# A gated layer and its FFN in one kernel: early items of the down stage one step sooner, fold transposes handed out with their block's first product, byte stores ordered behind sums

## The chip, the cores and the metric

The kernel runs on one core of a Trainium2 chip. Its engines are named as in the profile: PE (TensorE matmul), PEld (its weight load), DVE (VectorE), ACT (ScalarE), POOL (GpSimd), SP (SyncE, which issues the DMAs). The metric is the device time of one execution in microseconds (us), as the median of several runs.

## The reference, cut to what matters

There are 2 x 1024 rows of H = 1024, in float32. A gated layer with a top-k mask comes first, then an FFN whose weights are repeated four times and carry an addition of rank 2. A layer norm follows each.

```python
s = silu(x @ w_gate.T)                       # rows x 2752
_, idx = top_k(-abs(s), 2752 // 2)           # the half that is smallest in size
s[rows, idx] = 0
x = layernorm(x + (s * (x @ w_up.T)) @ w_down.T)

def lin(x, wq, A, B):                        # w is wq side by side four times
    return x @ tile(wq, (1, 4)).T + (x @ A.T @ B.T) * 0.5
x = layernorm(x + lin(silu(lin(x, w1q, a1, b1)) * lin(x, w3q, a3, b3), w2q, a2, b2))
```

## The kernel before, in words

**Numbers as pairs.** Each float32 operand of a product is split in a high part and a low part (`wh`, `wl`; `xh`, `xl`; `mh`, `ml`; `fh`, `fl`; `hh`, `hl`). Three products (high by high, high by low, low by high) stand for one. ACT or POOL writes a high part (`split`, L171 and L173 for weights), POOL or DVE subtracts it from the whole for the low part (L174).

**Stage 1, `gate_up`,** takes about 929 us. The 16 tiles of 128 rows go in four groups `g` of four tiles, the 2752 columns in four pairs `u` of blocks of 344. Each (g, u) has gate steps (w = "g", seven products of block matrices, or eight for the first) and up steps (w = "u", k = 0 to 3). A step of `products` is 96 matmuls of 344 columns (L353). Results go through DRAM: `s_d` for the gate, `m_d` for gate times up (L387). Between the steps a generator `topk(g - 1)` hands out the work that finds the k-th size in each row; it ends with a byte mask for each tile that SP stores to `k_d` (L539).

**Early items.** In the last up steps (g = 3, u = 3) the generator `down(0, early=3)` is started and stepped: it loads, masks and transposes the first 512 columns of three tiles into tiles of their own, `em`, `eh`, `el` (`self.et`), so that stage 2 finds its first three items ready. `down_prep` makes four transposes an item (L745), ACT copies them to `eh` (L749), DVE subtracts to `el` (L750).

**Stage 2, `down`,** lasts from 929 to about 1466 us: four groups of four tiles, and in each six blocks of columns (`DB`: 512, 512, 512, 384, 384, 448). An item is one tile in one block: load of `m` (L710) and of the byte mask `u` (L711), ACT's conversion `ub` (L724), POOL's multiplication (L725), transposes (L745, L747), products of 512 columns (L765), and DVE's addition to `acc` (L768), which was loaded with x (L775). The weights `wd` are loaded at L603, split, and in the first group stored as pairs (L679). The top-k work of the last group runs beside the first groups of this stage, on ACT and DVE. The PSUM tiles named `mm` come from a pool of three.

**Stage 3, `ffn(g)`,** lasts to the end. As the FFN's weights repeat four times, a row's four quarters are added first: `f1_tile` loads the row tile, folds it on POOL (L927 to L929, buffer `fold`, one of it) and writes a small tile `tl` with the rank-2 terms (L938 to L940, one buffer); for tiles 12 to 15 it also makes the four dot products of the rank-2 term (DVE L925, buffer `pr`, and ACT L926). `f1_tile2` transposes both (PE L949, L951), and ACT and DVE write `fh` (L954) and `fl` (L955). Then come eight blocks `b` of 344 columns: `f1_mm` makes seven products for each of gate and up (L981 to L984), silu (L987), their product (L988), its rank-2 terms (L990, L992), and POOL adds blocks of the same parity to `hf` (L994). Last, `f2_prep` transposes `hf` (L1026, L1031) into `hh` (L1028) and `hl` (L1029), and `f2_mm` makes the second product (L765), the norm and the store. In group g the `f1_tile` and `f1_tile2` of group g + 1's tiles are called, one of each in every second block.

**What sets the order.** `item(load, prep, mm, a1, a2)` calls `load` at once and hands out `prep` and `mm` later: an item waits behind `a1` others for its `prep`, and then behind `a2` others for its `mm`. In the FFN's first product both are 2, so the products of a tile are handed out four items, which is one block, after the block's loads. What is called outside an item is handed out where the program stands, ahead of the products still in the queues. But the order in which the instructions stand on each engine at the end is not that of the calls: a scheduler that plays the program's time line through writes it, within the dependences and the buffers. `issue_after` (with `load_behind` and `behind`) adds only an order between two instructions: `load_behind` puts an instruction behind the last load of `m`, `behind` puts it behind the last split of a down item on DVE and ACT.

Of the kernel before, what the change touches and what calls it, by code (L numbers as in the profile page):

```python
# [26 lines left out]
NU = NB // 2  # L27
# [5 lines left out]
GT = 4  # L33
# [32 lines left out]
class Kern:  # L66
# [216 lines left out]
    def gate_up(self):  # L283
        nc, V = self.nc, self.nc.vector
        ng = self.nt // GT
        self.steps = [(g, u, w, k) for g in range(ng) for u in range(NU) for w in "gu" for k in range(7 if w == "g" and g + u else 4)]
        self.xfull, self.tkg, self.xs, self.xraw, self.wraw, self.wq, self.li, self.wi = {}, None, {}, {}, [], [], 0, 0
        cc, self.b0 = {}, {}
        pss = {}
        xg = self.x_raw(0)  # L290
        next(xg)
        for i, (g, u, w, k) in enumerate(self.steps):
            while self.li < min(i + LOADS + 1, len(self.steps)):
                self.w_load(self.li)
                if self.li == 0:
                    list(xg)
                self.li += 1
            while self.wi < min(i + AHEAD + 1, len(self.steps)):
                j = self.steps[self.wi]
                if j[:2] == (0, 0):  # L300
                    for op in {("g", 0): ("A11", "A21"), ("g", 1): ("A12", "A22")}.get(j[2:], ()):
                        self.x_slot(op)
                self.w_prep(self.wi)
                self.wi += 1
            wh, wl = (x.rearrange("p (a b) -> p a b", a=KH) for x in self.wq.pop(0))
            if self.form(i):
                a = GATE[k][0]
                ps = self.pair()[:, :, :BW]
                self.products([(ps[:, p], self.xs[p, a]) for p in range(NPR)], wh, wl, True, True)
                self.post((g, u), k, ps, cc)  # L310
            else:
                first = w == "g"
                h = int((G0 if first else UP)[k][1]) - 1
                n = int((G0 if first else UP)[k][2]) - 1
                st, sp = (k < 2, k > 1) if first else (h == 0, h == 1)
                if st:
                    ps = [self.pair()[:, :, :BW] for j in range(2)]
                    pss[n] = ps
                ps = pss[n]
                for j in range(2):  # L320
                    self.products([(ps[j][:, p], self.xs[p, f"A{j + 1}{h + 1}"]) for p in range(NPR)], wh, wl, st, sp)
                if sp:
                    (self.up if w == "u" else self.gate)((g, u), n, ps, cc)
            if g + u == 0 and w == "u" and k:
                with self.behind():
                    for op in (("S2",), ("S1", "S3"), ("S4",))[k - 1]:
                        self.x_slot(op)
            if u == NU - 1 and g + 1 < ng:
                if (w, k) == XAT["raw"][0]:
                    self.xg = self.x_raw(g + 1)  # L330
                for _ in range(XAT["raw"].count((w, k))):
                    next(self.xg, None)
                for op in XAT.get((w, k), ()):
                    with self.behind():
                        self.x_slot(op)
            if g and (u, w, k) == TKAT:
                self.tkg = self.topk(g - 1)
            for _ in range(2 if w == "u" and k % 2 == 0 else 1):
                if self.tkg:
                    next(self.tkg, None)  # L340
            if (g, u, w) == (ng - 1, NU - 1, "u") and k > 1:
                next(self.d0)
            if (g, u, w, k) == (ng - 1, NU - 1, "u", 1):
                self.et = [self.tk.tile([P, NI], d, tag=f"a{j}", name=n) for j, (n, d) in enumerate((("em", F), ("eh", R), ("el", R)))]
                self.d0 = self.down(0, early=3)
                next(self.d0)
# [70 lines left out]
    def topk(self, g, nact=3):  # L417
        nc, tk, sm = self.nc, self.tk, self.sm
        V = nc.vector
        tiles = range(g * GT, (g + 1) * GT)  # L420
# [5 lines left out]
        b = ku.rearrange("p a n -> p (a n)").bitcast(F)  # L426
# [26 lines left out]
        for p in range(NPASS):  # L453
            for j in range(nact):
# [3 lines left out]
                with self.behind():  # L458
                    t, s = cur[:, 0, j : j + 1], cur[:, 1, j : j + 1]
                    nc.scalar.activation(jk.bitcast(I8), av[j], AF.Sign, bias=t, scale=-1.0, accum_out=s)  # L460
                    if m < GT:
                        t, s = cur[:, 0, m : m + 1], cur[:, 1, m : m + 1]
# [14 lines left out]
            t = nxt[:, 0]  # L477
# [57 lines left out]
        self.lastd = self.lastv = self.lasta = self.lastp = None  # L535
        for j, t in enumerate(tiles):
            yield
            with self.tc.issue_after(self.lastd.ins) if self.lastd is not None else ExitStack():
                nc.sync.dma_start(self.k_d[t], kv[j])  # L539

    def exact(self, a, kp, b, v, x, c, bit, half):
# [312 lines left out]
    def ffn(self, g):  # L854
        tiles = [t for t in range(g * GT, (g + 1) * GT) if t < self.nt]
        for b in range(NB):
            ws = []
            if tiles[-1] + 1 < self.nt:
                if b % 2 == 0:
                    if b:  # L860
                        self.f1_tile2(tiles[-1] + b // 2)
                    self.f1_tile(tiles[-1] + 1 + b // 2)
            for t in tiles:
                self.item(
                    lambda: self.f1_prep(b, ws),
                    lambda: None,
                    lambda st=self.fst[t], b=b, ws=ws: self.f1_mm(st, b, ws),
                    2, 2,
                )
        if tiles[-1] + 1 < self.nt:  # L870
            self.f1_tile2(tiles[-1] + GT)
        ws = []
        for t in tiles:
            self.item(
                lambda: self.f2_w(ws),
                lambda t=t: self.f2_prep(self.fst[t], t),
                lambda st=self.fst[t], t=t, ws=ws: self.f2_mm(st, t, ws),
                2, 1,
            )

# [211 lines left out]
```

## Time and profile before

| | |
|---|---|
| median of 3 runs | 1923.64 us (1919.69 to 1924.59) |
| the profiled execution's own time | 1926.91 us |
| its span, first to last instruction | 1925.1 us |
| mean granted TensorE clock | 0.993 |
| PE busy | 1885.3 us (98%), 10825 instructions |
| DVE, ACT, POOL busy | 1229.6, 904.0, 973.0 us |
| moved by DMA | 488.66 MB, mean 254 GB/s |

The span is that of one profiled execution and is compared with that execution's own time, not with the median. A share of busy time is a mean over three stages that have different limits, so the stretch around a change has to be looked at by itself: by a table of windows, by the waits with what released them, and by the timeline. "PEclk" is the share of full clock that TensorE was granted. Where a wait is for several things, the profile names the one that came last by its records.

### The profile page before, as it was taken

To read this page: it belongs to the slowest core of one execution; us is meant where nothing else is said; L and a number is where in the kernel's file an instruction comes from. 1 tells how busy PE (TensorE), PEld (TensorE's weight loads), DVE (VectorE), ACT (ScalarE), POOL (GpSimd) and SP (SyncE) were. 2 spreads that over 40 slices of the span, in tenths; PEclk is the share of its full clock that TensorE was granted. 3 is DMA by queue.
4 is the path that set the end of the run, shared out by engine and by line. 5 is a ranking of instruction groups with operands and counts; after the bars stand their busy time and mean duration, and the time that the engine had idled before them with its cause. 6 is when DMAs were issued, how large, how long until landed. Compare 5 with 4: busy or idle time off the path is not lost. (4 is left out here: it accounts for less than half of the span.)

```text
span 1925.1 us, 29381 instructions
## 1 busy us (share of the span) xinstructions
PE 1885.3 (98%) x10825; PEld 1754.4 (91%) x10825; DVE 1229.6 (64%) x1831; ACT 904.0 (47%) x1448; POOL 973.0 (51%) x606
## 2 busy tenths in 40 slices
PE   9999999999999999999999999999998999998998
PEld 9999999999999999999888787888787979898896
DVE  4633556767358574691238998688467857779565
ACT  4333477414883258622246533323333746557362
POOL 5655664445445354355565443554565746436062
PEclk9999999999999999999999999999999999999999
DMA  7677687676977868667798756977776878485651
GB/s 266 237 250 260 236 325 261 210 272 253 330 231 241 314 235 303 236 228 256 282 328 285 270 188 227 337 245 261 268 250 244 279 284 321 155 318 177 229 196 66
DMA packets 166205, 488.66 MB, mean 254 GB/s; under 512 B 24772, under 2 KB 45380, under 8 KB 166056
## 3 DMA queue, kind: packets, MB, share of 16 engines
q1 hardware_dynamic: 165848, 486.43, 71.9%
q8 instruction: 85, 1.39, 0.3%
q14 instruction: 64, 0.52, 0.1%
q10 hardware_dynamic: 208, 0.31, 0.0%
HBM read 370.30 MB, written 116.33 MB: 253 GB/s over the span
## 5 line engine op out<-in xcount | busy, mean ns | idle before, releaser
L174 POOL TENSOR_TENSOR wl<-wr,wh 128x1376 fp32r<-128x1376 f32 (+2 forms) x187 | 566.4, 3035 | 466.1 <-ACT wh L173 436.8
L353 PE MATMUL mm<-wh,xh 128*128 128x344 f32 x1928 | 610.4, 322 | 2.8 <-DMA wh<-tw3T1h 2.8
L353 PE MATMUL mm<-wh,xl 128*128 128x344 f32 x1928 | 609.8, 320 | 0.0
L173 ACT CAST wh<-wr 128x1376 fp32r<-128x1376 f32 (+2 forms) x192 | 232.4, 1215 | 340.9 <-PE mm L353 199.6
L353 PEld LDWEIGHTS mm<-wh,xh 128*128 128x128 f32 x1928 | 364.7, 189 | 3.0 <-issue 3.0
L353 PEld LDWEIGHTS mm<-wh,xl 128*128 128x128 f32 x1928 | 364.6, 189 | 0.0
L353 PE MATMUL mm<-wl,xh 128*128 128x344 f32 x1928 | 342.1, 319 | 0.0
L353 PEld LDWEIGHTS mm<-wl,xh 128*128 128x128 f32 x1928 | 310.1, 188 | 0.0
L765 PE MATMUL mm<-wh,mh 128*128 128x512 f32 x680 | 217.8, 400 | 0.1
L765 PE MATMUL mm<-wl,mh 128*128 128x512 f32 x680 | 215.1, 395 | 1.1 <-POOL wl L174 1.1
L765 PE MATMUL mm<-wh,ml 128*128 128x512 f32 x648 | 205.5, 396 | 0.8 <-DVE ml L750 0.8
L460 ACT ACTIVATE jk<-a,cur 128x2752 int8<-128x2752 f32 x66 | 170.8, 2588 | 31.2 <-DVE cur L482 15.8
L994 POOL TENSOR_TENSOR hf<-hf,gt 128x344 f32<-128x344 f32 x96 | 142.2, 1491 | 75.6 <-DVE gt L988 68.7
L725 POOL TENSOR_TENSOR m<-m,ub 128x512 f32<-128x512 f32 (+2 forms) x93 | 111.0, 1194 | 128.0 <-ACT ub L724 65.8
L981 PE MATMUL mm<-wh,fh 128*128 128x344 f32 x512 | 166.2, 325 | 5.8 <-DVE gt L988 5.2
L983 PE MATMUL mm<-wh,fl 128*128 128x344 f32 x512 | 164.0, 320 | 0.0
L982 PE MATMUL mm<-wl,fh 128*128 128x344 f32 x512 | 163.9, 320 | 0.0
L765 PEld LDWEIGHTS mm<-wl,mh 128*128 128x128 f32 x680 | 127.4, 188 | 30.1 <-POOL wl L174 2.2
L768 DVE TENSOR_TENSOR acc<-acc,mm 128x1024 f32<-128x1024 f32 x96 | 116.4, 1214 | 57.9 <-PE mm L765 27.8
L765 PEld LDWEIGHTS mm<-wh,mh 128*128 128x128 f32 x680 | 124.7, 189 | 24.8 <-ACT mh L749 0.5
L765 PEld LDWEIGHTS mm<-wh,ml 128*128 128x128 f32 x648 | 121.2, 189 | 26.9 <-DVE ml L750 1.0
L992 ACT ACTIVATE pa<-pa 128x344 f32<-128x344 f32 x256 | 123.0, 483 | 38.6 <-DVE pa L990 34.0
(191 smaller groups left out, 2742.5 us busy)
## 6 DMA issues: line engine op xcount, KB each, us to landing
wr<-wu SPq DMA_DIRECT2D x64, 688.0 KB
wr<-wg SPq DMA_DIRECT2D x52, 688.0 KB
wr<-wd SPq DMA_DIRECT2D x48, 512.0 KB
s_d<-cc SPq DMA_DIRECT2D x64, 344.0 KB
m_d<-mt SPq DMA_DIRECT2D x64, 344.0 KB
a<-s_d SPq DMA_DIRECT2D x64, 344.0 KB
wl<-wc_w SPq DMA_DIRECT2D x48, 344.0 KB
wh<-wc_w SPq DMA_DIRECT2D x48, 344.0 KB
```

What stands on the lines that cost most here:

```text
L173: self.lasta = self.nc.scalar.copy(hi, raw)
L174: (eng or self.nc.gpsimd).tensor_tensor(lo, raw, hi.bitcast(F), ALU.subtract)
L353: self.nc.tensor.matmul(o, l, r, start=start and n < m and n % (2 * KH) == 0, stop=stop and n >= m and (n - m) % KH == KH - 1)
L460: nc.scalar.activation(jk.bitcast(I8), av[j], AF.Sign, bias=t, scale=-1.0, accum_out=s)
L725: nc.gpsimd.tensor_tensor(m[:, :w], m[:, :w], ub[:, :w], ALU.mult)
L765: nc.tensor.matmul(ps[:, h], a, b[:, h * 512 : (h + 1) * 512], start=i == 0, stop=i == len(ops) - 1)
L768: nc.vector.tensor_tensor(out, out, ps.rearrange("p a b -> p (a b)"), ALU.add)
L981: nc.tensor.matmul(o, fh[:, c, :], wh[:, c, :], start=c == 0, stop=False)
L982: nc.tensor.matmul(o, fh[:, c, :], wl[:, c, :], start=False, stop=False)
L983: nc.tensor.matmul(o, fl[:, c, :], wh[:, c, :], start=False, stop=False)
L992: nc.scalar.activation(pa[:, r], pa[:, r], AF.Copy, scale=0.5, accum_out=part[:, r, b : b + 1])
L994: G.tensor_tensor(hf[:, hs], hf[:, hs], gt, ALU.add)
```

## The change

Three edits. In `gate_up` the early generator is made at k = 0 and stepped at k = 1 and 2, where it was made at k = 1 and stepped at k = 2 and 3. In `topk` the store of a byte mask is ordered behind the last load of `m` and behind the last split of a down item on DVE and ACT, where it was ordered behind the load alone. In `ffn` the calls of `f1_tile2` and `f1_tile` for the next group's tiles are put in a list `pre`, and the first product of the block that is handed out calls what is in it; the last `f1_tile2` is called with the first product of `f2_mm`. The same functions are called, with the same arguments. In the file after the change the lines from `ffn` on have numbers lower by one.

```diff
-            if (g, u, w) == (ng - 1, NU - 1, "u") and k > 1:
+            if (g, u, w) == (ng - 1, NU - 1, "u") and k in (1, 2):
                 next(self.d0)
-            if (g, u, w, k) == (ng - 1, NU - 1, "u", 1):
+            if (g, u, w, k) == (ng - 1, NU - 1, "u", 0):
                 self.et = [self.tk.tile([P, NI], d, tag=f"a{j}", name=n) for j, (n, d) in enumerate((("em", F), ("eh", R), ("el", R)))]
                 self.d0 = self.down(0, early=3)
                 next(self.d0)
...
         for j, t in enumerate(tiles):
             yield
-            with self.tc.issue_after(self.lastd.ins) if self.lastd is not None else ExitStack():
+            with self.load_behind(), self.behind():
                 nc.sync.dma_start(self.k_d[t], kv[j])
...
         for b in range(NB):
             ws = []
-            if tiles[-1] + 1 < self.nt:
-                if b % 2 == 0:
-                    if b:
-                        self.f1_tile2(tiles[-1] + b // 2)
-                    self.f1_tile(tiles[-1] + 1 + b // 2)
+            pre = []
+            if tiles[-1] + 1 < self.nt and b % 2 == 0:
+                if b:
+                    pre.append(lambda b=b: self.f1_tile2(tiles[-1] + b // 2))
+                pre.append(lambda b=b: self.f1_tile(tiles[-1] + 1 + b // 2))
             for t in tiles:
                 self.item(
                     lambda: self.f1_prep(b, ws),
                     lambda: None,
-                    lambda st=self.fst[t], b=b, ws=ws: self.f1_mm(st, b, ws),
+                    lambda st=self.fst[t], b=b, ws=ws, pre=pre: ([pre.pop(0)() for _ in pre[:]], self.f1_mm(st, b, ws)),
                     2, 2,
                 )
-        if tiles[-1] + 1 < self.nt:
-            self.f1_tile2(tiles[-1] + GT)
+        pre = [lambda: self.f1_tile2(tiles[-1] + GT)] if tiles[-1] + 1 < self.nt else []
         ws = []
         for t in tiles:
             self.item(
                 lambda: self.f2_w(ws),
                 lambda t=t: self.f2_prep(self.fst[t], t),
-                lambda st=self.fst[t], t=t, ws=ws: self.f2_mm(st, t, ws),
+                lambda st=self.fst[t], t=t, ws=ws, pre=pre: ([pre.pop(0)() for _ in pre[:]], self.f2_mm(st, t, ws)),
                 2, 1,
             )
```

## The prediction

> **What bounds the kernel now.** I read the page first, then the waits of TensorE, then a table by windows, then the timeline where a window is low.
>
> ```profile
> PE 1885.3 (98%) x10825; PEld 1754.4 (91%) x10825; DVE 1229.6 (64%) x1831; ACT 904.0 (47%) x1448; POOL 973.0 (51%) x606
> ```
>
> TensorE is busy 98% of 1925.1 us; the rest, 39.8 us, is all that moving work can win, plus what the halved clock costs. Where it lies:
>
> ```profile
> core 0: us, PE busy (x) PEld busy (x) DVE busy (x) ACT busy (x) POOL busy (x), PEclk, DMA share, GB/s
> ...
> 930.00:950.00 20.00, 16.66 (x69) 13.28 (x68) 4.76 (x7) 6.05 (x10) 13.72 (x8) 0.83 0.96 359
> ...
> 1050.00:1100.00 50.00, 48.70 (x229) 39.73 (x228) 48.39 (x91) 28.43 (x33) 20.31 (x16) 1.00 0.77 284
> ...
> 1450.00:1500.00 50.00, 45.10 (x238) 40.04 (x237) 38.95 (x97) 24.41 (x58) 24.24 (x33) 0.93 0.72 250
> ...
> 1550.00:1600.00 50.00, 47.19 (x233) 39.55 (x232) 30.27 (x74) 17.97 (x48) 15.87 (x25) 0.97 0.76 297
> ...
> 1700.00:1750.00 50.00, 48.09 (x309) 47.52 (x308) 48.51 (x74) 38.48 (x117) 27.63 (x25) 1.00 0.80 275
> ```
>
> The row 930–950, where stage 2 begins, loses most: PE busy 16.66 of 20, clock 0.83. 1450–1500 and 1550–1600 are FFN rows. In 1050–1100 and 1700–1750 the column DVE is 48.4 of 50: no room there. What ends the waits:
>
> ```profile
> PE mm L765 <- ACT hh L1028: 4.4, 3, 2.8
> PE tp L745 <- POOL m L725: 4.3, 2, 2.7
> PE tp L949 <- POOL fold L929: 3.2, 2, 1.9
> PE mm L745 <- DVE el L750: 1.9, 1, 1.9
> ```
>
> And the timeline at the start of stage 2, then at the FFN's start (start, length, engine and line, and in brackets the idle time before and its releaser):
>
> ```profile
> 929.54 1.03 PE L745 MATMUL mm<-ident,em 128*128 128x128 f32 x8
> 932.47 0.63 PE L745 MATMUL mm<-ident,em 128*128 128x128 f32 x4 [1.90 <-DVE el L750]
> 934.54 1.19 PE L765 MATMUL mm<-wh,eh 128*128 128x512 f32 x2 [1.45 <-POOL wl L174]
> 935.54 1.05 PE L765 MATMUL mm<-wl,eh 128*128 128x512 f32 x2
> ...
> 1481.06 0.44 PE L949 MATMUL tp<-ident,fold 128*128 128x128 f32 x2 [1.87 <-POOL fold L929]
> ...
> 1482.23 0.42 PE L981 MATMUL mm<-wh,fh 128*128 128x344 f32 x1 [0.51 <-DVE hf L988]
> ```
>
> The last up product starts at 929.4; then come the twelve transposes of the early items, in two lots, and the first down product at 934.54. The releaser "POOL wl" of that one is a guess of the view: in the built program it needs the third el from DVE (933.75–934.44), which needs eh, which needs the last four transposes.
>
> **The change, part by part.** Both built programs have equal counts of instructions on each engine. Their orders differ in two stretches only, about 922 to 1115 us and from 1478 on.
>
> **1. Early items one k sooner.** Eight of the twelve transposes move ahead of the second-last group of 24 products, four to six products into the last. ACT's eh and DVE's el follow them at about 923–927; they have all they need (their masks ended at 906 on POOL, the PSUM buffer was released at 915.55). The last el is done some 2 us before the last up product. So the first down product follows products: 929.54 + 12 x 0.109 (a transpose at its step) = 930.85, in place of 934.54: -3.69. Then the clock: the seven pairs of 512-column products from 934.54 on take 6.05 us to 940.59, where at the 0.231 step of full clock 14 need 3.23: -2.82 if the halved clock goes too.
>
> Here a rule speaks against the change. The Trainium skill, "TensorE: Matmul & The Clock Gate", Part 1: The HAM clock gate, says that the clock is halved after at least one idle window of about 3.4 us, and the table in its "Why this matters for your kernels" asks only for no gap over some 3 us. The row has 1.90 and 1.45, so by this rule the clock did not fall for these gaps, and -2.82 is not to be had. But its Part 4: PE-mode transpose says that transposes don't count as busy in the same way; then all from 929.54 to 934.54 is one quiet stretch of 5.0 us. The trace sides with that: clock 0.5 from 933.7 to 940.5, and a single gap of 2.7 us at 1188 with products on both sides left it at 1.00. In the new order eight transposes in a row are 0.87 us. I take -2.82; by the first rule the sum below is 2.8 worse.
>
> New wait: PE now reaches the fourth down item, which needs an mm buffer back, after 72 products and 8 transposes: 930.85 + 17.5 = 948.4. The buffer is freed by DVE's L768, which took 1.22 us and waits for the load acc<-x: issued at 940.72, landed at 947.04 (6.3 us, with the DMA engines at 0.96). In the new order that issue stands behind a weight load that waits for POOL's last splits, which wait for the last up product: about 1.1 later. So 948.1 + 1.2 = 949.4: +1.0 (0 to 3).
>
> Behind this the queues differ: on SP the wd loads come ahead of m, u and topk's a<-s_d (L440), on ACT and POOL the splits (L173, L174) stand ahead of the masks (L724, L725) that were before them, by 5 to 10 us. Following the chains by hand to 985, I find POOL's masks done 4 to 8 us ahead of their transposes: m at 956.9 for 961.8, 962.9 for 967.9, 968.4 for 976. Behind 1050 DVE is the narrow place: 97% busy, with topk passes of 3.07 us (L463) between the adds L768 (1.21) that free PSUM. There PE may have to hand back what it won. Bounds 0 and +5.5; I take +1, as TensorE still waited only 1.3 us in that window.
>
> Sum of part 1: -3.7 - 2.8 + 1.0 + 1.0 = -4.5.
>
> **2. Byte stores of the top-k bound.** The stores L539 stand in the same place on SP with the same waits in both built programs: 0. Were they moved, 64 KB loads u<-k_d are what waits for them, in other groups' masks.
>
> **3. Folds with the first product.** The code asks for all four fold groups of the next tiles later, but the written order moves just the last group of each block of four tiles: on PE from 1481 to about 1565, 1615 to 1672, 1722 to 1773. The first move doesn't pay on the spot: the product at 1482.23 needs DVE's hf (1481.66), and DVE's work ahead of it stays, so instead of 1.87 + 0.44 + 0.51 there is one gap of about 3.0, with the clock still halved; and four transposes (0.44) come back among products in f2. What it may win is at f2's start, where PE waits 2.81 for hh at 1554.62: ACT's fh (L954, 0.6) and DVE's fl (0.41) now stand behind hh. So hh is 0.6 to 1.0 sooner, and 1.8 of half clock behind that gap may go: -0.6 to -2.8. Group 1: 0 (its gap is 1.3). Group 2: the same 0.6 to 1.0, against the dots of tiles 13 to 15 (L925, four of 1.2 us a tile) that go one block later where DVE has no room: -1 to +3. I take -1.5 for all three, range -4 to +3. Cover: POOL and ACT are under 80% there; DVE is not, and that is the upper end.
>
> **Sum:** -4.5 + 0 - 1.5 = -6.0, against the profiled execution's own 1926.9 (span 1925.1 and 1.8 around it). That execution lies 3.3 over the median of 1923.64, and a shift carries over: 1917.6. About 0.3% (5.8 us) is what a measurement of this kernel can tell from no change, so this stands on the edge.
>
> **The rivals.**
> **Handed back** (chance 0.30). PE arrives 5.5 us sooner at a stage whose adds and masks are paced by DVE at 97% and by DMA at 0.96 and 0.91. For: those columns. Against: PE's own busy time in 950–1050 is 100%, so nothing was late there. If all of it goes back: +5.5 against the -6.5 +1.0, and the FFN's -1.5 stays: 1922.1.
> **The change doesn't do what it says** (inside both cases above). Two of its three parts nearly fall away in the written order; then part 1 alone carries it: 1919.1.
> **Slower: DVE's new order in 1000–1115** (chance 0.22). Where the topk passes fall differently, an add L768 can stand behind one more pass of 3.07 us, and PE, which has three mm buffers, stops until it is done. For: 1050–1100 has DVE at 48.39 of 50, and that stretch is rewritten. Against: with DVE as full as that, PE lost 1.5 us at 1072 in the order before, and nothing else between 1000 and 1115. Each such stop costs up to 3.07; beyond -6.0 the forecast turns at the second, and slower by 0.3% needs four. Five give +15.4 - 6.0 = +9.4, or with stops of 2.7, as the one at 1188, +7.5: 1931.
>
> **How the numbers follow.** Gain kept, -5.8 to -12 (chance 0.48): the upper end is no hand-back, no acc wait, and FFN -4. Handed back, within 0.3%: 0.30. Slower: 0.22. Range: below, 1911 is the forecast less the two +1 terms, and the FFN at -4, with a margin of 2 (0.07 left out); above, 1930 is just short of five stops (0.12 left out).
>
> **What would show it.** Right: ident,em in two lots ahead of 929, the first L765 at about 931, no clock of 0.5 in 933–940, and window 930–950 with PE over 19. The acc wait: PE before the fourth item's L765 idle about 1 us, released by L768. FFN: a gap of about 3 at 1479 less the shift; hh's 2.81 down to 2 or less. Wrong: clock 0.5 still there at the start of stage 2, or new lines "PE mm L765 <- DVE acc L768" of several us in 1000–1115, or hf and hh lines longer in the third FFN block.

## The result, and the profile after

The changed kernel takes 1930.95 us (median of 6 runs, 1927.42 to 1933.56), before takes 1921.51 us (6 runs, 1919.08 to 1924.59): ratio 1.0045, 95% interval 1.0031 to 1.0058. It is slower by some 9 us. The forecast was 1917.6.

The profiled execution of the changed kernel, at 1927.63 us, is one of its quickest, and that of before, at 1926.91 us, lay over all its six timed runs, so the two spans hardly differ. PE is still 98% busy (1885.5 us). So it has to be read stretch by stretch. The windows of the changed kernel, with the columns as above:

```profile
930.00:950.00 20.00, 20.00 (x98) 16.83 (x96) 1.57 (x2) 5.97 (x8) 14.08 (x8) 1.00 0.90 339
950.00:1000.00 50.00, 48.40 (x230) 39.58 (x229) 18.91 (x21) 21.30 (x29) 29.79 (x18) 1.00 0.94 347
1000.00:1050.00 50.00, 47.00 (x217) 37.87 (x217) 31.96 (x48) 29.87 (x36) 31.14 (x26) 1.00 0.79 277
...
1700.00:1750.00 50.00, 47.24 (x297) 46.06 (x297) 45.81 (x70) 38.02 (x115) 26.22 (x24) 1.00 0.74 245
1750.00:1800.00 50.00, 45.63 (x239) 39.49 (x238) 38.29 (x68) 26.66 (x82) 19.12 (x22) 0.97 0.38 124
```

Three of these windows before:

```profile
950.00:1000.00 50.00, 50.00 (x236) 41.03 (x235) 16.28 (x18) 19.34 (x27) 28.35 (x18) 1.00 0.91 328
1000.00:1050.00 50.00, 50.00 (x236) 40.95 (x236) 38.93 (x58) 31.63 (x40) 35.53 (x29) 1.00 0.86 292
...
1750.00:1800.00 50.00, 46.59 (x255) 40.91 (x254) 37.78 (x68) 27.39 (x84) 20.23 (x24) 1.00 0.41 128
```

In 930–950 PE is now busy all the time at full clock: what the forecast was after is there. But 950–1000 and 1000–1050, where PE lacked nothing before, lose 1.6 and 3.0 us, and both FFN windows lose about 0.9 more each; the last of them has lost full clock too (0.97). What ends PE's waits in the changed kernel:

```profile
PE mm L765 <- ACT hh L1027: 6.7, 3, 3.2
PE mm L980 <- DVE gt L987: 6.0, 8, 1.1
PE mm L765 <- ACT mh L749: 3.9, 4, 1.9
...
PE mm L980 <- DVE hf L987: 2.7, 1, 2.7
PE mm L765 <- DVE acc L768: 1.6, 1, 1.6
```

"el" and "m" are gone from the top; "mh" and "acc" are new, and "hh" has grown from 4.4. The timeline of PE shows each in its place:

```profile
929.47 0.60 PE L745 MATMUL mm<-ident,em 128*128 128x128 f32 x4
...
932.74 0.63 PE L765 MATMUL mm<-wh,eh 128*128 128x512 f32 x2
...
951.98 0.70 PE L765 MATMUL mm<-wh,mh 128*128 128x512 f32 x2 [1.60 <-DVE acc L768]
...
1023.88 0.73 PE L765 MATMUL mm<-wh,mh 128*128 128x512 f32 x2 [0.57 <-ACT mh L749]
...
1033.47 0.82 PE L745 MATMUL tp<-ident,m 128*128 128x128 f32 x6
1036.15 0.73 PE L765 MATMUL mm<-wh,mh 128*128 128x512 f32 x2 [1.86 <-ACT mh L749]
```

The first down product no longer waits (no bracket at 932.74). At 951.98 PE waits for its PSUM tile. From 1023 on an item's transposes stand right ahead of its products, and PE has nothing to do until ACT has written mh. Two of these waits, of 0.57 us, are the way over ACT alone. In the longest, 1.86 us at 1036.15, a load has a part as well. ACT's cast of a weight stands ahead of mh in ACT's order, and ACT sat idle for 2.54 us until the weight was there:

```profile
1034.68 1.04 ACT L173 CAST wh<-wr 128x1024 fp32r<-128x1024 f32 x1 [2.54 <-DMA wr<-wd]
1035.63 0.86 ACT L749 CAST mh<-tp 128x384 fp32r<-128x384 f32 x2
```

**One measure for all runs.** Below, "loss" is the sum, over PE's instructions in a stretch, of the time from one start to the next less the usual step of that shape (0.109, 0.157 and 0.231 us for 128, 344 and 512 columns). It holds idle time and halved clock alike; a stretch without a wait comes out at about -0.1. Each row is one profiled execution:

| kernel | 929–944 | 944–1020 | 1020–1060 | 1060–1120 | 1466–1562 | 1690–1790 |
|---|---|---|---|---|---|---|
| before | 6.5 | -0.1 | -0.1 | 1.5 | 13.6 | 7.4 |
| byte stores alone (before's order) | 5.3 | -0.1 | -0.1 | 1.4 | 15.1 | 7.5 |
| changed | 0.0 | 1.7 | 3.8 | 1.4 | 14.4 | 11.7 |
| changed, again | 0.0 | 4.0 | 4.5 | 1.4 | 14.2 | 11.5 |
| early edit alone | 0.0 | 3.7 | 5.4 | 1.4 | 13.9 | 7.5 |
| FFN edit alone | 6.4 | -0.1 | -0.1 | 1.9 | 14.7 | 11.6 |

The first two rows have one order of instructions, and so have rows three and four: they show what differs between executions of one order. Between 1120 and 1466, where the order is before's in all these kernels, the six executions differ by some 6 us in this measure (6.0 to 12.3), and no cause was read from there.

### The profile page after: what moved, and what is told of

Same layout as the page of the kernel before. It is cut to its first block, busy times and chain, and to the rows that moved or that the text cites. A ratio compares the mean times of both kernels' runs of the same rounds, so it can differ in the third digit from the quotient of the medians.

```text
span 1925.8 us, 29383 instructions
## 1 busy us (share of the span) xinstructions
PE 1885.5 (98%) x10825; PEld 1755.8 (91%) x10825; DVE 1223.8 (64%) x1831; ACT 905.9 (47%) x1448; POOL 974.0 (51%) x606
## 5 line engine op out<-in xcount | busy, mean ns | idle before, releaser
L460 ACT ACTIVATE jk<-a,cur 128x2752 int8<-128x2752 f32 x66 | 170.8, 2588 | 33.8 <-DVE cur L490 18.3
```

## The experiments

Times are medians. Ratios, with 95% intervals, are against runs of before on the same chip, whose medians are 1922.99 to 1923.57 us; a ratio differs by up to 0.0007 from that of the two medians. "F", "H" and so on are the theories that the expectations name.

**1. The parts, one by one.**

*The early edit alone:*

```diff
-            if (g, u, w) == (ng - 1, NU - 1, "u") and k > 1:
+            if (g, u, w) == (ng - 1, NU - 1, "u") and k in (1, 2):
...
-            if (g, u, w, k) == (ng - 1, NU - 1, "u", 1):
+            if (g, u, w, k) == (ng - 1, NU - 1, "u", 0):
```

> Before, with the first edit alone (early items made at k = 0, stepped at k = 1 and 2). Theory F (the loss lies in the FFN): this is faster than before by 2 to 6 us, about 1917, and its trace has no PE loss from 930 to 948 and the new one of about 6 us between 948 and 1115. Theory H (what is won at 930 is handed back twice over behind it): 3 to 9 us slower, 1925 to 1930.

Measured: 1925.38 us, ratio 1.0014 (1.0006 to 1.0022), slower by about 2.7. Theory F's time (about 1917) is ruled out, and theory H's is met at its lower edge (1925 to 1930): the gain is handed back and a little more, not twice over. Its waits from 929 to 1100, for which before's order has only el, wl and ml:

```profile
PE mm L765 <- ACT mh L749: 3.8, 4, 1.9
PE mm L765 <- DVE acc L768: 2.1, 1, 2.1
```

*The FFN edit alone* (the `pre` lists, as in the change):

```diff
-                    lambda st=self.fst[t], b=b, ws=ws: self.f1_mm(st, b, ws),
+                    lambda st=self.fst[t], b=b, ws=ws, pre=pre: ([pre.pop(0)() for _ in pre[:]], self.f1_mm(st, b, ws)),
```

> Before, with the FFN edit alone. Theory F: slower by 6 to 12 us, 1928 to 1933, with PE losing 5 us or more over before's 21.5 us from 1470 on. Theory H: within 2 us of before.

Measured: 1927.91 us, ratio 1.0028 (1.0019 to 1.0037), +5.4: most of the loss is the FFN's. That is just short of theory F's 6 to 12 and outside theory H's 2, so the loss has a share in both places.

*The byte stores alone:*

```diff
-            with self.tc.issue_after(self.lastd.ins) if self.lastd is not None else ExitStack():
+            with self.load_behind(), self.behind():
                 nc.sync.dma_start(self.k_d[t], kv[j])
```

> Before, with the edit of the byte stores alone. On each engine the order of instructions and their waits are those of before, so every theory expects 1921 within 2 us; it also gives a second profile of what is before's program, and so shows how far two executions of one order differ. If stores count after all: slower by over 5 us.

Measured: 1923.43 us, ratio 1.0000 (0.9989 to 1.0010). This part does nothing. Its profile serves below as a second one of before's order.

*The changed kernel on the same chip:*

> The changed kernel as it is, on the chip of the three others. 9 us slower than before (1930 to 1931); if the parts add up, its difference is the sum of those of the early edit and of the FFN edit within 3 us.

Measured: 1932.40 us, ratio 1.0042 (1.0024 to 1.0060). The parts add up: +0.0014 and +0.0028 give +0.0042.

**2. Why the early edit loses: lead.** In the written order of PE I counted the instructions between an item's last transpose and its first product, for the first twenty items after the early ones:

```
before               40 63 62 63 81 64 62 76 79 56 70 65 57 57 51 48 55 41 48 62
early edit, changed  10 29 45 21 25 40 44 61 67 57 51 32 18  1  1  4  5 10 27 23
```

Before, 40 or more instructions of PE cover the way from transpose over ACT to product. With the early edit the lead falls to 1 at the 14th item, and there, at 1023 to 1036, PE waits for mh. Why the scheduler's order has come to this was not followed. Theory L is that this is the loss; theory A, that PE has merely caught up with loads. The top-k work of the last group enters ACT's queue at item 12 of the group. Beginning it at item 16 restores the leads (10 29 45 21 25 40 47 64 70 82 76 67 61 61 57 57 57 30 25 36):

```diff
-                if g == 0 and n == 12:
+                if g == 0 and n == 16:
...
-                if (n > 11 or g) and self.tkg and next(self.tkg, 1):
+                if (n > 15 or g) and self.tkg and next(self.tkg, 1):
```

> The early edit alone, and the top-k work of the last group begins at item 16 of the first down group and not at item 12, so that its ACT passes come after the items that lost their lead. In the written order transposes then stand 30 to 80 PE instructions ahead of their products, where the early edit alone left 1 to 5 at items 14 to 17. Theory L (late transposes are what gives the gain back): the three waits for mh at 1024 to 1035 are gone, PE's loss from 948 to 1120 falls from 7.6 to 4 or less, time 3 to 5 us under the early edit alone, about 1921. Theory A (PE has only caught up with loads, whatever the order): the loss stays at 6 or more, time 1925.

> Before, with the top-k work begun at item 16 and not at item 12: the control for the run with the early edit. Leads there are long already, so both theories expect 1923 within 2 us; if beginning later pays or costs by itself, it shows here.

Measured: 1939.20 us with the early edit (1.0076, 1.0063 to 1.0089), 1944.43 us without (1.0106, 1.0091 to 1.0120). The expected times were wrong: beginning top-k later costs about 20 us by itself, much of it behind 1120: the loss from there to 1430 is 18.3 us in the control and 26.5 with the early edit (the slowest of its five runs), against 7.5 in the first profile of before. But against its own control the early edit now wins 5 us (1.0076 / 1.0106 = 0.9970), and from 930 to 1100 the waits for mh are gone:

```profile
PE mm L765 <- DVE acc L768: 2.7, 1, 2.7
PE tp L745 <- DVE num L488: 0.5, 1, 0.5
```

The loss at 1020–1060 is 0.0. Theory A would have kept it. What is left is the wait for acc, with 6.8 us of halved clock behind it, and it is large: 944–1020 loses 5.7. So from 948 to 1120 the loss is 6.5, where theory L wanted 4 or less, and from 929 to 1120 the two profiles lose the same (6.4 and 6.6). Where the 5 us are won doesn't show in them.

**3. Both losses taken out.** An item waits behind four others for its products in the first group (its transposes come one item sooner), and the first two acc loads are no longer ordered behind the loads of m:

```diff
-                    self.item(lambda: (load(), self.down_w(g, ib, ws)), prep, mm, 2, 3)
+                    self.item(lambda: (load(), self.down_w(g, ib, ws)), prep, mm, 2, 3 if g else 4)
...
-            with self.tc.issue_after(self.lastd.ins) if self.lastd is not None else ExitStack():
+            with self.tc.issue_after(self.lastd.ins) if self.lastd is not None and t > 1 else ExitStack():
                 self.nc.sync.dma_start(acc, self.A["x"][t * P : (t + 1) * P, :])
```

> The early edit alone, and in the first down group an item waits behind four others for its products, not three, so that transposes are handed out one item sooner; the top-k work begins where it did. Leads in the written order are 14 to 77 PE instructions, one of 6, in place of 1 to 67. Theory L (short leads): the waits for mh around 1024 to 1035 fall from 5.4 us to under 2, time about 1922. Theory A (caught up with loads): 1925 as with the early edit alone.

Measured, first edit on top of the early one: 1925.40 us, ratio 1.0003 (0.9991 to 1.0014). The time is theory A's number, the trace is not: the loss at 1020–1060 fell from 5.4 to 0.8, as theory L says, although ACT sat idle there for 3.6 us on the load of a weight; the longer lead covered that. But 1060–1120 rose from 1.4 to 6.5 (in the slowest of its 14 runs): there a top-k pass (L463) now stands on DVE ahead of ml and acc:

```profile
1079.31 3.07 DVE L463 TENSOR_SCALAR_CACHE_REDUCE ku<-a,cur 128x2752 uint8<-128x2752 f32 x1
...
1083.09 1.21 DVE L768 TENSOR_TENSOR acc<-acc,mm 128x1024 f32<-128x1024 f32 x1
1084.23 0.68 DVE L750 TENSOR_TENSOR ml<-tp,mh 128x512 fp32r<-128x512 f32 x1
```

and PE waits 1.56 us for that ml, with 6.8 us of halved clock.

> The early edit alone, and the first two loads acc<-x are not ordered behind the loads of m: on SP they stand 13 places sooner. The wait for acc L768 at about 950 (2.1 us, with the 1.5 to 1.9 us of halved clock behind it) goes, leads stay short (1 at items 15 and 16). Both theories expect 2 to 4 us under the early edit alone, about 1922.5, unless PE, let go at 950, then waits for mh there (the leads of the first two items are 5): then 1925.

Measured, second edit on top of the early one: 1923.31 us, ratio 0.9994 (0.9983 to 1.0005). The loads went out at 930.63 and 934.35, where the changed kernel has them at 943.84 and 944.91; the wait for acc and its halved clock are gone (944–1020: 0.3). Leads stay short and the loss there stays too (1020–1060: 7.1, of waits for mh and ml and 6.8 us of halved clock).

> Both of these on top of the early edit: the two acc loads sooner, and an item waits behind four others in the first down group. Theory L: nothing much is left of the loss behind 948, so PE's gain at 930 is kept: 1918 to 1920, faster than before by 3 to 5 us. Theory A: 1923 to 1925.

Measured, both: 1918.17 us, ratio 0.9968 (0.9956 to 0.9981): faster than before by about 6 us and than the changed kernel by about 14. Leads are 5 5 18 25 26 37 49 62 60 56 63 49 47 17 22 23 15 10 27 27. Its windows:

```profile
930.00:950.00 20.00, 20.00 (x98) 16.86 (x97) 4.03 (x5) 4.87 (x6) 12.90 (x7) 1.00 0.96 345
950.00:1000.00 50.00, 48.80 (x233) 39.75 (x232) 16.46 (x19) 22.89 (x32) 31.79 (x20) 1.00 0.98 363
1000.00:1050.00 50.00, 50.00 (x234) 40.81 (x233) 35.15 (x56) 29.88 (x36) 32.38 (x28) 1.00 0.82 288
```

The gain at 930 is there and 1000–1050 is whole again. It is what theory L expected (1918 to 1920). The two repairs together without the early edit were not run.

> Before, with four in place of three in the first down group: the control. Its leads were 40 to 80 and stay so: 1923 within 2 us.

Measured, the first edit on before: 1932.20 us, ratio 1.0045 (1.0026 to 1.0064). The control failed its expectation: with leads of 23 to 94 it is 9 us slower. 1060–1120 loses 5.1 (PE waits 2.2 for ml, behind a top-k pass again) and 1120–1300 loses 7.8, with one wait of 4.7 us for a mask; the latter is read in a single profile. So four in place of three is not good in itself, and a long lead is not all that counts.

**4. Why the FFN edit loses.** Group 2 differs from the others in that the tiles folded during it have dots on DVE, of 1.2 us each.

> Before, with the FFN edit in group 2 of the FFN alone (the one whose next tiles 12 to 15 need dots on DVE). Theory D (the dots one block later are the cost): +3 to +5 us over before, about 1927, with PE losing 11.5 us from 1690 to 1790 in place of 7.6. Theory G (each group costs its share): +1 to +2.

> Before, with the FFN edit in all groups but group 2. Theory D: within 1.5 us of before, the group-0 start losing 1.3 us more (longer halved clock) and its second product winning as much. Theory G: +3 to +4 us, about 1926.5.

```diff
     def ffn(self, g):
+        if g == 2:                     # the other run: g != 2
+            return self.ffn_new(g)     # the changed kernel's ffn
```

Measured: group 2 alone 1926.76 us, ratio 1.0017 (1.0009 to 1.0025), loss at 1690–1790 11.3; the other groups 1924.11 us, 1.0003 (0.9994 to 1.0012), loss 6.6. The cost sits in group 2, as theory D has it. Then the two calls in group 2 one at a time:

```diff
                     if g == 2:
+                        pre.append(lambda b=b: self.f1_tile(tiles[-1] + 1 + b // 2))
                     # the other run: f1_tile2, and the last of it with f2_mm, as in the change
```

> Before, with only f1_tile (the fold, and for tiles 13 to 15 of the next group the dots on DVE) of FFN group 2 handed out with the first product; its transposes f1_tile2 are called as before. Theory D (the dots one block later are the cost): the +3.3 us of the edit in group 2 is all here, about 1926.5, PE's loss from 1690 to 1790 at 11 or more. Theory T (the transposes moved among products are the cost): 1923.5, loss 7.6.

> Before, with only the transposes f1_tile2 of FFN group 2 handed out with the first product (the last with the first of f2), f1_tile called as before. Theory D: 1923.5 within 1.5, loss from 1690 to 1790 about 7.6; as a tile's transposes are then behind and there is one buffer fold, the next tile's fold can still be held back, and with it its dots: then up to +3. Theory T: 1926.5.

Measured: `f1_tile` 1925.36 us, ratio 1.0013 (1.0002 to 1.0025), loss 11.0; `f1_tile2` 1922.13 us, 0.9999 (0.9989 to 1.0010), loss 8.6. The fold with its dots carries what can be measured; the transposes alone cost at most 2 us. The fold was not run apart from the dots. In the changed kernel the dots of two tiles run on DVE so:

```profile
1735.74 1.95 DVE L924 TENSOR_TENSOR pr<-x2a,abc 128x1024 f32<-128x1024 f32 x1
...
1738.03 3.08 DVE L924 TENSOR_TENSOR pr<-x2a,abc 128x1024 f32<-128x1024 f32 x2
...
1741.45 1.21 DVE L924 TENSOR_TENSOR pr<-x2a,abc 128x1024 f32<-128x1024 f32 x1
...
1762.45 1.21 DVE L924 TENSOR_TENSOR pr<-x2a,abc 128x1024 f32<-128x1024 f32 x1
```

In before's order (the profile with the byte stores alone) it is

```profile
1726.97 4.76 DVE L925 TENSOR_TENSOR pr<-x2a,abc 128x1024 f32<-128x1024 f32 x3
...
1732.50 1.74 DVE L925 TENSOR_TENSOR pr<-x2a,abc 128x1024 f32<-128x1024 f32 x1
...
1753.38 1.21 DVE L925 TENSOR_TENSOR pr<-x2a,abc 128x1024 f32<-128x1024 f32 x1
```

The last dots end at 1754.6 there and 9 us later in the changed kernel, closer to f2. The waits of PE from 1700 to 1790, first in before's order, then changed, then (from 1720 on) with `f1_tile2` alone:

```profile
PE mm L981 <- DVE gt L988: 3.6, 4, 1.9
PE mm L765 <- ACT hh L1028: 0.9, 1, 0.9
```

```profile
PE mm L980 <- DVE gt L987: 4.9, 7, 0.9
PE mm L765 <- ACT hh L1027: 2.2, 1, 2.2
```

```profile
PE mm L765 <- ACT hh L1033: 2.5, 1, 2.5
```

The earlier tile's three dots in a row became one, two, one with a gt between, so PE waits for gt seven times, not four: 1.3 us. And hh at the start of f2 is waited for 1.3 us longer. That wait does not need late dots: it is 2.5 us with the transposes alone handed out late, where the dots stand as before. What differs is the clock behind it. In all five profiles with `f1_tile` of group 2 late, 3.41 us of halved clock (a loss of 1.7) begin within 1.5 us of the end of that wait; in the one with `f1_tile2` alone there is none. So the place of the loss and the call that brings it are shown. How it divides between dots, fold and clock is not.

## Why the prediction was wrong

- **First down product and clock, -6.5: right.** 929–944 lost 5.2 to 6.5 us in before's order and loses nothing in any execution of the early edit; no stretch of halved clock stands at 933–940. Both products and clock came. The reason given for the clock is not shown by that: elsewhere single gaps of 1.96 and 2.09 us, which by that rule should not cost the clock, were followed by halved clock (last section). So the gap of 1.90 may have been enough, without the transposes. And the gap of 2.7 us that was held against it (it lies at 1191.7 to 1194.4, not at 1188) kept full clock in that one execution.
- **acc wait, +1.0 (0 to 3): place and releaser right, too small.** It waits 1.6 to 2.5 us: the load took 6.8 us from its issue at 943.84 to the addition that waited for it, not 6.3 (counted from the first down product, PE's arrival and the issue are where they were put); and in two of the three profiles 3.4 us of halved clock follow it. I had taken the halved clock off at 933 and not asked whether the new wait brings it back. The stretch costs 1.8 to 4.1.
- **What else is handed back, +1.0 (0 to 5.5): the step that failed, with the one on the FFN.** It cost 3.9 to 5.5 us at 1020–1060. I followed the masks by hand to 985, found them 4 to 8 us ahead, and put the rest on DVE behind 1050. The loss lies between the two, and it is not the masks that are waited for but mh, the step from transpose over ACT to product, for which the sum had no term. The number that would have told it, the lead of each item's transposes in the written order, was to be had from the program: it falls from 40 or more to 1.
- **Handed back** as a rival came near the sum of part 1 (nothing kept, against +2.7 measured), but its first reason, DVE at 97%, is not what happened: 1060–1120 lost no more than before. Its second, the DMA, has the part shown at 1036. The stops behind a top-k pass, the mechanism of the slower rival, did appear, in the two runs with four items ahead, not in the changed kernel. That the rival's 1931 is the measured time is chance: its cause was another.
- **Byte stores, 0: right.**
- **FFN, -1.5 (-4 to +3): wrong, +5.4 (1.0028).** At the start of group 0 the gap is 2.68, as forecast (3.0), but the halved clock behind it lasted 6.8 us where both profiles of before's order have 3.4. At f2 the gain was forecast with the wrong sign: hh is waited for 3.21, not 2.0, and before it was 2.81; in group 2 the wait grows from 0.9 to 2.2. That handing the transposes out later brings hh sooner is the step that failed; why it comes later was not followed. Over 1466–1562 the edit costs nothing that stands out (14.2 to 14.7 against 13.6 and 15.1). Group 2 was bounded at +3 and sits at 3.3 (1.7 to 4.8): I saw that DVE had no room there and still took -1.5 for the sum. About 1.5 us of the edit's 5.4 is not placed; it is within the intervals.
- **The base:** the median of before in the later experiments is 1923, so a shift from the first median was fair.
- **Two slips.** The row 930–950 loses most by share only: by the measure above 1450–1500 loses 9.6 us, 930–950 6.5. And the terms named for the upper end of the gain add up to -10.5; -12 has the margin of 2 in it.

## What to carry to other kernels

When work is pulled ahead under a scheduler that rewrites the order, count in the written program how far each producer stands ahead of its consumer, over the whole stage behind the edit: most of the time won at the edit here was lost again 90 us later, at leads of one instruction. A long lead is not all: the run with four items ahead and no early edit had leads of 23 or more and lost 9 us. Moving work later can cost as well: 20 us for the top-k work, 3.3 for the folds of group 2. Where an edit wins at its own place and loses elsewhere, repair the loss before dropping the edit: with two loads sooner and one more item ahead the early edit gave 0.9968 of before.

## What the runs showed of the hardware

The same gap in PE's work, in the same order of instructions around it, was followed by halved clock in one execution and not in another. At 1192 to 1196 PE waits for m ahead of four transposes: after 2.70 us (before) the clock stayed at 1.00; after 1.96 (changed, again), 2.09 (FFN edit outside group 2) and 2.78 us (`f1_tile` of group 2) it was 0.5 for 3.41 us. At 950 the wait for acc kept full clock after 1.60 us and lost it for 3.41 us after 2.08 and 2.50. So in this range the length of a single gap doesn't decide; what does, these runs don't show. With one order of instructions, PE lost between 6.0 and 12.3 us from 1120 to 1466 in six executions, so the first profile of each kernel shows spans that differ by only 0.7 us, where the medians differ by 9.
